# Last groups of a graph layer taken half by half, and products of zeros moved to another bank

## The chip, the cores and the metric

One core of one Trainium2 chip runs the whole kernel. The metric is the device time of one execution in microseconds (us); the median of three runs of the kernel before is 2110.1 us (2109.29 to 2110.33).

The engines, by the short names of the profile: PE multiplies matrices (PEld loads its weights), DVE works on vectors, ACT applies functions, POOL issues the gathers from memory, SP issues the other transfers. Each engine takes its instructions strictly in the order in which they were written for it. Between engines, an instruction waits for semaphores: the end of a write that it needs, or the end of the last use of a buffer that it is to overwrite.

## The reference

Two layers of graph attention with a normalisation ahead and two dense layers behind, added to the input: 6250 nodes with 768 numbers each, 100000 edges sorted by their destination, and one loop edge for each node.

```
h = relu(layernorm(x))
h = relu(gat_conv(h, src, dst, W1, a_src1, a_dst1, b1, heads=4))   # layer 1, 768 -> 256
h = relu(gat_conv(h, src, dst, W2, a_src2, a_dst2, b2, heads=1))   # layer 2, 256 -> 256
h = relu(h @ Wm1 + bm1)
out = x + (h @ Wm2 + bm2)

def gat_conv(x, src, dst, W, a_src, a_dst, bias, heads):
    h = (x @ W).reshape(n, heads, -1)
    alpha_s, alpha_d = (h * a_src).sum(-1), (h * a_dst).sum(-1)
    e = leaky_relu(alpha_s[src] + alpha_d[dst], 0.2)
    e = exp(e - segment_max(e, dst)[dst])
    alpha = e / (segment_sum(e, dst)[dst] + 1e-16)
    return segment_sum(h[src] * alpha[:, :, None], dst) + bias
```

## The kernel before

The 6250 nodes are 49 tiles of 128 (NT = 49). The 100000 edges are 782 tiles of 128, the last with 32 edges. Four edge tiles make a *group* (TPG = 4; NG = 196 groups, numbers 0 to 195, and group 195 has only two tiles), two tiles of a group a *half* or pair, and two groups a *sum* (NU = 98 sums, numbers 0 to 97), which is one accumulation in a bank of PE's result memory, `o_ps`. Such banks rotate: the tag "o" has three of them. Layer 1 is computed first, then layer 2, and nothing of the change touches layer 1.

What layer 2 does with one group, in `group`: POOL has gathered, for each edge, the row of its source node into `G` (256 features, the exponentials of its score, a one for the denominator). DVE has made `hot`, which is 1 where edge and destination match (`make_hot`, L704, for the next group or the next but one). `rho_ps` holds a row per destination, one of four slots for each sum, written by PE (`meet`, L720). In the whole form DVE multiplies `rho_ps` by a column of `G` into `u_ps` (L773), takes the maximum with another column (L775), both for two tiles at a time, and multiplies `hot` by `u_ps` for all four (L778): five instructions. Then PE adds the four products hot x G into the sum (L780). In the other form (`last=True`) it goes tile by tile: one instruction multiplies and takes the maximum (L767), one multiplies `hot` (L769), and that tile's product can follow.

Around it, for each group g, the loop writes `pair(g, 0)`, then one step of the dense layers of earlier nodes, the taking up of a sum, `make_hot` for a later group, other steps, and then `pair(g, 1)`. In layer 2 `pair` runs `group` on the whole group at p == 1 and does nothing at p == 0, but for the last two groups, 194 and 195. `take_sum` (L818, `acc`) reads a finished sum from its bank and adds what it shares with the sum before it; two sums finish a node tile on ACT (L827). Which sum is taken up where stands in UP_AT by hand: sum 95 after the first half of group 192. A node tile then goes through `Node2.steps`: add the loop edge (L1143), divide by the denominator (L1155, L1158), transpose (L1001), ACT (L1007), first dense layer (L1167), ACT (L1172), second dense layer in two parts of 384 columns (L1116 adds the bias, L1177), each part added to x by DVE (L1181), and out. One bank `y_ps` serves both parts in turn, so that PE starts the second when DVE has read the first.

The end is written out in `last_pairs`: sum 96 is taken up, then PE multiplies zeros (`stay_warm`, L902) into the two slots of `rho_ps` that sums 96 and 97 don't use, the halves of groups 194 and 195 follow, and between them the steps of the last two node tiles, 47 (`before`) and 48 (`last`).

Of the kernel before, what the change touches and what calls it, by code (L numbers as in the profile page):

```python
# [10 lines left out]
F32 = mybir.dt.float32  # L11
# [6 lines left out]
P = 128  # L18
# [12 lines left out]
NG = NQ  # L31
# [5 lines left out]
NU = NG // 2  # L37
# [34 lines left out]
def kernel(  # L72
# [21 lines left out]
    nc = tc.nc  # L94
# [9 lines left out]
    ps = edges_stack.enter_context(tc.tile_pool(name="ps", bufs=2, space=bass.MemoryType.PSUM))  # L104
# [28 lines left out]
    idle = const.tile([P, 4 * P], BF16, name="idle")  # L133
# [507 lines left out]
    def layer_edges(layer, H, node, pre, matched, pre_pool):  # L641
# [4 lines left out]
        with tc.tile_pool(name=f"eg{layer}", bufs=6) as eg, \  # L646
# [7 lines left out]
            else:  # L654
                u_ps = ps.tile([P, TPG, P], F32, name="u_ps", tag="factors", bufs=1)
                rho_ps = ps.tile([P, 4, P], F32, name="rho_ps", tag="parts", bufs=1)

            def tiles(g):

                return range(max(TPG * g, FIRST) - TPG * g, min(TPG * g + TPG, LAST) - TPG * g)  # L660
# [89 lines left out]
            def sums_of(u):  # L750

                if u not in o_ps:
                    o_ps[u] = ps.tile([P, RW[layer]], F32, name="o_ps", tag="o", bufs=3)
                return o_ps[u]

            def group(g, of, last=False):

                of = [k for k in of if k in tiles(g)]
                if not of:
                    return  # L760
                u, pairs = g // 2, sorted({k // 2 for k in of})
                row = rho_ps[:, u % 4]
                Gs = {p: G.pop(TPG // 2 * g + p) for p in pairs}
                if last:
                    for k in of:
                        Gk = Gs[k // 2][:, k % 2]
                        nc.vector.tensor_scalar(u_ps[:, k], row, Gk[:, HID + 2:], Gk[:, HID:HID + 1],  # L767
                                                ALU.mult, ALU.max)
                        nc.vector.tensor_mul(hot[g][:, k], hot[g][:, k], u_ps[:, k])  # L769
                else:  # L770
                    for p in pairs:
                        at = slice(2 * p, 2 * p + 2)
                        nc.vector.tensor_mul(u_ps[:, at], row.unsqueeze(1).to_broadcast([P, 2, P]),  # L773
                                             Gs[p][:, :, HID + 2:].to_broadcast([P, 2, P]))
                        nc.vector.tensor_max(u_ps[:, at], u_ps[:, at],  # L775
                                             Gs[p][:, :, HID:HID + 1].to_broadcast([P, 2, P]))
                    at = slice(of[0], of[-1] + 1)
                    nc.vector.tensor_mul(hot[g][:, at], hot[g][:, at], u_ps[:, at])  # L778
                for k in of:
                    nc.tensor.matmul(sums_of(u), hot[g][:, k], Gs[k // 2][:, k % 2, :RW[2]],  # L780
                                     start=(g % 2 == 0 and k == 0),
                                     stop=(g % 2 == 1 and k == tiles(g)[-1]))

            def pair(g, p):

                if layer == 2:
                    if g >= NG - 2:
                        group(g, (2 * p, 2 * p + 1), True)
                    elif p == 1:
                        group(g, range(TPG))  # L790
                    return
                if 2 * p not in tiles(g):
                    return
                Gp = G.pop(TPG // 2 * g + p)
                e1, e2 = Gp[:, :, RW[1]:RW[1] + 4], Gp[:, :, RW[1] + 4:]
                at = TPG * (g % 4) + 2 * p
                rho, v, w = (e_ps[g // 4][:, at:at + 2, k * H:(k + 1) * H] for k in range(3))
                nc.vector.tensor_mul(v, e2, rho)  # L798
                nc.vector.tensor_max(w, v, e1)  # L799
                hw = hwp.tile([P, 2, H, C + 1], F32, name="hw")  # L800
                nc.vector.tensor_mul(  # L801
                    hw, Gp[:, :, :RW[1]].rearrange("p t (h c) -> p t h c", h=H),
                    w.unsqueeze(3).to_broadcast([P, 2, H, C + 1]))
                for t in range(2):
                    k = 2 * p + t
                    nc.tensor.matmul(sums_of(g // 2), hot[g][:, k], hw[:, t].rearrange("p h c -> p (h c)"),  # L806
                                     start=(g % 2 == 0 and k == 0),
                                     stop=(g % 2 == 1 and k == tiles(g)[-1]))
# [3 lines left out]
            def take_sum(u):  # L812

                acc = sums.tile([P, RW[layer]], F32, name="acc")
                if u == 0:
                    nc.vector.tensor_copy(acc, o_ps.pop(u))
                else:
                    nc.vector.scalar_tensor_tensor(acc, run[0], keep[:, u % 2:u % 2 + 1],  # L818
                                                   o_ps.pop(u), ALU.mult, ALU.add)
                for Q in (2 * u - 1, 2 * u):  # L820
                    t, q = divmod(Q, 4)
                    if not 0 <= t < NT - 1:
                        continue
                    if q == 0:
                        done[t] = sums.tile([P, RW[layer]], F32, name="sum", bufs=3)
                    r = slice(32 * q, 32 * q + 32)
                    nc.scalar.activation(done[t][r], acc[r], AF.Copy)  # L827
                    if q == 3:
                        late.append(node.steps(t, done.pop(t)))
                        begun[late[-1]] = t  # L830
                run[0] = acc
                return acc

            def carry_over(acc):

                nc.vector.memset(acc[96:], 0.0)
                run[0] = node.whole(NT - 1, acc)
# [56 lines left out]

            def last_pairs():

                free = 2 * (1 - (NU - 1) % 4 // 2)
                idle_ps = rho_ps[:, free:free + 2].rearrange("p u n -> p (u n)")

                def stay_warm(n):  # L900
                    for _ in range(2 * n):
                        nc.tensor.matmul(idle_ps, idle[:, :P], idle[:, :2 * P], start=True, stop=True)  # L902

                acc = take_sum(NU - 2)
                before, = late
                stay_warm(8)
                pair(NG - 2, 0)
                next(before)
                carry_over(acc)
                next(before)  # L910
                stay_warm(2)
                next(before)
                pair(NG - 2, 1)
                next(before)
                pair(NG - 1, 0)
                pair(NG - 1, 1)
                last = node.steps(NT - 1, None, run[0], o_ps.pop(NU - 1))
                for of in (last, before, last, before, last, before, before, last, last):
                    next(of, 0)
                late.clear()  # L920

            for g in range(NG):
                t, j = divmod(g, 4)
                if layer == 2 and g >= NG - 2:
                    if g == NG - 2:
                        last_pairs()
                    continue
# [594 lines left out]
```

## Time and profile before

| | |
|---|---|
| median of three runs | 2110.1 us (2109.29 to 2110.33) |
| the profiled execution | 2106.61 us, of it 2104.6 us span from the first to the last instruction |
| PE busy | 1649.6 us, 78% of the span |
| DVE busy | 1609.2 us, 76% |
| POOL busy | 1527.1 us, 73% |
| ACT busy | 442.3 us, 21% |
| granted PE clock, mean | 0.917 |

In the rows of the profile a line gives the start in us from the first instruction, the time that the instructions took, the engine, the line of the kernel, the operation, what is written from what, and how many stand together; in square brackets the engine's idle time just before, and what ended it. A matrix product of fp32 numbers appears as two MATMUL records, so that "x8" is four products of a group. Most of the time is spent in the two loops over the groups; the part that this change touches is the last 45 us.

### The profile page before, as it was taken

The page shows a single profiled execution, that of the slowest core. Times are in us where ns is not written, and L with a number is a line of the kernel's source. Part 1 is how long each engine was busy: PE and PEld are TensorE (multiplying, and loading weights), DVE is VectorE, ACT ScalarE, POOL GpSimd, SP SyncE. Part 2 cuts the span into 40 slices and gives each one's busy share as a digit, 9 for nine tenths or more (in the row PEclk, how much of TensorE's full clock was granted, in tenths as well). Part 3 has the DMA queues.
Part 4 walks back from the last instruction along what each step waited for, and adds up shares of the span by engine and source line. Part 5 has one row for each costly group of instructions (what it writes and reads, how often), then busy time and mean ns, then how long its engine had stood idle before and what let it go on. Part 6 is the DMA issues. An engine that isn't in the chain of part 4 may idle for free.

```text
span 2104.6 us, 24738 instructions
## 1 busy us (share of the span) xinstructions
PE 1649.6 (78%) x7217; PEld 1217.7 (58%) x7218; DVE 1609.2 (76%) x3795; ACT 442.3 (21%) x1388; POOL 1527.1 (73%) x1666
## 2 busy tenths in 40 slices
PE   8986879877887887887763787777877777776776
PEld 6875657655665665665542555555555555554554
DVE  7857788887888888888773877777877777776764
ACT  5761111111111111111120111111211111121211
POOL 7067777777777777777777777777777777777773
PEclk9997999998998999999885999998999999999898
DMA  9998455555555556555447355555545555554552
GB/s 349 348 347 286 143 157 155 157 147 155 162 155 149 156 156 161 151 147 161 132 124 215 107 159 159 146 149 159 149 147 159 159 146 149 159 152 137 153 162 77
DMA packets 145655, 354.68 MB, mean 169 GB/s; under 512 B 33943, under 2 KB 57582, under 8 KB 145510
## 3 DMA queue, kind: packets, MB, share of 16 engines
q0 software_dynamic: 75040, 210.90, 37.1%
q1 hardware_dynamic: 69100, 140.62, 19.9%
q10 hardware_dynamic: 1370, 1.48, 0.3%
q8 instruction: 59, 0.97, 0.2%
q14 instruction: 86, 0.70, 0.1%
HBM read 311.29 MB, written 41.59 MB: 168 GB/s over the span
## 4 chain that ended last, share of the span: by engine, by line
DVE 29%; PE 27%; DMA 23%; issue 12%; POOL 7%; ACT 1%; DVEq 0%; SPq 0%; POOLq 0%; ACTq 0%
DMA G<-table,src_i 20%; PE o_ps L780 11%; POOL G L679 7%; DVE u_ps L773 5%; DVE u_ps L775 5%; PE h_ps L471 4%; DVE hw L801 4%; DVE hot L704 4%; DVE hot L778 3%; PE y_ps L1177 2%; PE tp L1167 2%; PE missing L329 2%; DVE soon_hit L318 2%; PE o_ps L806 2%; PE missing L394 2%
## 5 line engine op out<-in xcount | busy, mean ns | idle before, releaser
L679 POOL DMA_INDIRECT G<-table,src_i x1498 | 1426.9, 953 | 456.3 <-issue 266.2
L780 PE MATMUL o_ps<-G,hot 128*128 128x258 f32 x1564 | 445.9, 435 | 245.9 <-DVE hot L778 244.8
L806 PE MATMUL o_ps<-hw,hot 128*128 128x260 f32 x1564 | 457.6, 431 | 170.4 <-DVE hw L801 152.5
L780 PEld LDWEIGHTS o_ps<-G,hot 128*128 128x128 f32 x1564 | 319.5, 213 | 366.1 <-DVE hot L778 313.6
L806 PEld LDWEIGHTS o_ps<-hw,hot 128*128 128x128 f32 x1564 | 302.4, 206 | 284.9 <-DVE hw L801 212.1
L827 ACT ACTIVATE sum<-acc 32x260 f32<-32x260 f32 (+1 forms) x384 | 160.0, 417 | 1345.4 <-DVE acc L818 1286.1
L773 DVE TENSOR_TENSOR u_ps<-rho_ps,G 128x256 f32<-128x256 f32 x388 | 166.5, 429 | 183.8 <-PE rho_ps L720 98.9
L801 DVE TENSOR_TENSOR hw<-G,factors 128x520 f32<-128x520 f32 x391 | 272.1, 696 | 41.3 <-DVE factors L799 2.3
L704 DVE TENSOR_TENSOR hot<-iota_ps,dcol 128x512 f32<-128x512 f32 x392 | 266.0, 679 | 0.0
L329 PE MATMUL missing<-kept,soon_hit 128*128 128x268 f32 x1028 | 246.6, 397 | 0.0
L329 PEld LDWEIGHTS missing<-kept,soon_hit 128*128 128x128 f32 x1028 | 199.8, 196 | 37.5
L775 DVE TENSOR_TENSOR u_ps<-u_ps,G 128x256 f32<-128x256 f32 x388 | 167.7, 432 | 13.4
L1177 PE MATMUL y_ps<-wm,mT 128*128 128x384 f32 x392 | 153.1, 514 | 0.3 <-ACT mT L1172 0.3
L798 DVE TENSOR_TENSOR factors<-G,factors 128x8 f32<-128x8 f32 x391 | 65.0, 166 | 102.8 <-DMA G<-table,src_i 98.5
L471 PE MATMUL h_ps<-w,r 128*128 128x264 f32 (+1 forms) x588 | 137.4, 387 | 7.2 <-ACT r L461 7.0
L778 DVE TENSOR_TENSOR hot<-hot,u_ps 128x512 f32<-128x512 f32 x194 | 133.1, 686 | 6.7
L471 PEld LDWEIGHTS h_ps<-w,r 128*128 128x128 f32 x588 | 107.8, 190 | 29.4 <-ACT r L461 10.6
L292 POOL DMA_INDIRECT G<-table,soon_i x46 | 44.0, 957 | 74.5 <-DMA xt<-in_x 53.0
L818 DVE SCALAR_TENSOR_TENSOR acc<-acc,keep,o_ps 128x260 f32<-128x260 f32 (+1 forms) x192 | 91.5, 477 | 7.8 <-PE o_ps L780 7.8
L1177 PEld LDWEIGHTS y_ps<-wm,mT 128*128 128x128 f32 x392 | 67.0, 191 | 44.3 <-issue 17.4
L799 DVE TENSOR_TENSOR factors<-factors,G 128x8 f32<-128x8 f32 x391 | 68.0, 174 | 13.6 <-DVE factors L798 0.2
L1181 DVE TENSOR_TENSOR y<-y_ps,xt 128x384 f32<-128x384 f32 (+1 forms) x98 | 54.0, 551 | 29.1 <-PE y_ps L1177 28.9
(426 smaller groups left out, 1367.9 us busy)
## 6 DMA issues: line engine op xcount, KB each, us to landing
xt<-in_x SPq DMA_DIRECT2D x96, 384.0 KB, 5.3
drow<-dmod_d SPq DMA_DIRECT2D x49, 512.0 KB, 5.2
G<-table,src_i POOLq DMA_INDIRECT x1498
xTt<-in_xT SPq DMA_DIRECT2D x49, 384.0 KB, 7.5
out<-y SPq DMA_DIRECT2D x48, 384.0 KB, 3.1
table<-kept SPq DMA_DIRECT2D x49, 134.0 KB, 5.3
table<-kept SPq DMA_DIRECT2D x49, 129.5 KB, 2.7
soon_d<-G SPq DMA_DIRECT2D x23, 268.0 KB, 7.9
```

Source lines behind the costliest of these rows:

```text
L329: nc.tensor.matmul(soon_p[k], hit[:, T - there], kept[T], start=(T == there), stop=(T == NT - 1))
L471: nc.tensor.matmul(h_ps[:, :n], r[:, k], w1[:, k, :n], start=(k == 0), stop=(k == KI - 1))
L679: nc.gpsimd.indirect_dma_start(out=G[k // 2][:n, k % 2], out_offset=None, in_=table[layer], in_offset=bass.IndirectOffsetOnAxis(ap=src_i[: ...
L704: nc.vector.tensor_tensor(hot[g][:, T[0]:T[0] + n], iota_ps.unsqueeze(1).to_broadcast([P, n, P]), dcol[:, k:k + n].unsqueeze(2).to_broadca ...
L773: nc.vector.tensor_mul(u_ps[:, at], row.unsqueeze(1).to_broadcast([P, 2, P]), Gs[p][:, :, HID + 2:].to_broadcast([P, 2, P]))
L775: nc.vector.tensor_max(u_ps[:, at], u_ps[:, at], Gs[p][:, :, HID:HID + 1].to_broadcast([P, 2, P]))
L778: nc.vector.tensor_mul(hot[g][:, at], hot[g][:, at], u_ps[:, at])
L780: nc.tensor.matmul(sums_of(u), hot[g][:, k], Gs[k // 2][:, k % 2, :RW[2]], start=(g % 2 == 0 and k == 0), stop=(g % 2 == 1 and k == tiles( ...
L801: nc.vector.tensor_mul(hw, Gp[:, :, :RW[1]].rearrange("p t (h c) -> p t h c", h=H), w.unsqueeze(3).to_broadcast([P, 2, H, C + 1]))
L806: nc.tensor.matmul(sums_of(g // 2), hot[g][:, k], hw[:, t].rearrange("p h c -> p (h c)"), start=(g % 2 == 0 and k == 0), stop=(g % 2 == 1 ...
L827: nc.scalar.activation(done[t][r], acc[r], AF.Copy)
L1177: nc.tensor.matmul(y_ps, mT[:, j], wm2[:, j, s * half:(s + 1) * half], start=False, stop=(j == KH - 1))
```

## The change

The whole diff:

```
-                    if g >= NG - 2:
+                    if g >= NG - 4:
                         group(g, (2 * p, 2 * p + 1), True)
                     elif p == 1:
                         group(g, range(TPG))
...
             def last_pairs():
 
-                free = 2 * (1 - (NU - 1) % 4 // 2)
-                idle_ps = rho_ps[:, free:free + 2].rearrange("p u n -> p (u n)")
+                idle_ps = ps.tile([P, 4 * P], F32, name="idle_ps", tag="o", bufs=3)
 
                 def stay_warm(n):
-                    for _ in range(2 * n):
-                        nc.tensor.matmul(idle_ps, idle[:, :P], idle[:, :2 * P], start=True, stop=True)
+                    for _ in range(n):
+                        nc.tensor.matmul(idle_ps, idle[:, :P], idle, start=True, stop=True)
```

Groups 192 and 193 are now also done in halves, tile by tile. The first half of group 192 comes ahead of the taking up of sum 95 and of two `make_hot`, and its products come ahead of the second dense layer of node tile 46 on PE. The products of zeros write to a bank of the tag "o", which is no longer a part of `rho_ps`; each is 512 columns wide in place of 256, and there are half as many. Because two lines are gone, the lines behind them have numbers that are lower by one.

Three places of the order of instructions follow. The names: `hot_15632` and `G_15581`, `G_15586` belong to group 192, `hot_15676` before and `hot_15683` now with `G_15654`, `G_15659` to group 194; `o_ps_15604` is sum 95; L1181 (now L1180) is the addition of x for node tiles 45 and 46. What a row waits for stands in brackets: DMASW is the gathers, DMAHW other transfers.

DVE around group 192, before:

```order
L1181 TENSOR_TENSOR y_15574<-y_ps_15575,xt_15404 128x384 [waits PE_49]
L818 SCALAR_TENSOR_TENSOR acc_15670<-acc_15589,keep_86,o_ps_15604 128x258 [waits PE_49]
L704 TENSOR_TENSOR hot_15674<-iota_ps_77,dcol_94 128x512
L704 TENSOR_TENSOR hot_15676<-iota_ps_77,dcol_94 128x512
L773 TENSOR_TENSOR u_ps_9898<-rho_ps_9899,G_15581 128x256 [waits DMASW7_49,DMASW6_49,DVE_49]
L775 TENSOR_TENSOR u_ps_9898<-u_ps_9898,G_15581 128x256 [waits DVE_49]
L773 TENSOR_TENSOR u_ps_9898<-rho_ps_9899,G_15586 128x256 [waits DMASW1_49,DMASW0_49,DVE_49]
L775 TENSOR_TENSOR u_ps_9898<-u_ps_9898,G_15586 128x256 [waits DVE_49]
L778 TENSOR_TENSOR hot_15632<-hot_15632,u_ps_9898 128x512 [waits DVE_49]
L1181 TENSOR_TENSOR y_15665<-y_ps_15666,xt_15521 128x384 [waits DMAHW6_49,DMAHW4_49,PE_49]
L678 MEMSET G_15694 128x259
L1181 TENSOR_TENSOR y_15665<-y_ps_15666,xt_15521 128x384 [waits PE_49]
```

The same twelve places of DVE now:

```order
L1180 TENSOR_TENSOR y_15574<-y_ps_15575,xt_15404 128x384 [waits PE_49]
L767 TENSOR_SCALAR u_ps_9898<-rho_ps_9899,G_15581 128x128 [waits DMASW6_49,DVE_49]
L769 TENSOR_TENSOR hot_15632<-hot_15632,u_ps_9898 128x128 [waits DVE_49]
L767 TENSOR_SCALAR u_ps_9898<-rho_ps_9899,G_15581 128x128 [waits DMASW7_49,DVE_49]
L769 TENSOR_TENSOR hot_15632<-hot_15632,u_ps_9898 128x128 [waits DVE_49]
L818 SCALAR_TENSOR_TENSOR acc_15677<-acc_15589,keep_86,o_ps_15604 128x258 [waits PE_49]
L704 TENSOR_TENSOR hot_15681<-iota_ps_77,dcol_94 128x512
L704 TENSOR_TENSOR hot_15683<-iota_ps_77,dcol_94 128x512
L767 TENSOR_SCALAR u_ps_9898<-rho_ps_9899,G_15586 128x128 [waits DMASW0_49,DVE_49]
L769 TENSOR_TENSOR hot_15632<-hot_15632,u_ps_9898 128x128 [waits DVE_49]
L767 TENSOR_SCALAR u_ps_9898<-rho_ps_9899,G_15586 128x128 [waits DMASW1_49,DVE_49]
L769 TENSOR_TENSOR hot_15632<-hot_15632,u_ps_9898 128x128 [waits DVE_49]
```

Five instructions on a whole group have become twice four on single tiles; the first four stand ahead of the taking up of sum 95 (L818), the others behind both `make_hot` (L704) and ahead of the addition of x.

PE around group 192, before (`o_ps_15683` before and `o_ps_15666` now are sum 96, `y_ps_15666` and `y_ps_15673` the second dense layer of node tile 46):

```order
L1167 MATMUL tp_15629<-rT_15645,wm1_9850 128x128 [waits Activation_49]
L1167 MATMUL tp_15629<-rT_15645,wm1_9850 128x128 x3
L1116 LDWEIGHTS ones_r_9854
L1116 MATMUL y_ps_15666<-bm2r_9853,ones_r_9854 128x384 [waits DVE_49]
L1177 MATMUL y_ps_15666<-wm2_9851,mT_15662 128x384 [waits Activation_49] x2
L780 MATMUL o_ps_15683<-G_15581,hot_15632 128x258 [waits DMASW6_49,DVE_49]
L780 MATMUL o_ps_15683<-G_15581,hot_15632 128x258 [waits DMASW7_49]
L780 MATMUL o_ps_15683<-G_15586,hot_15632 128x258 [waits DMASW0_49]
L780 MATMUL o_ps_15683<-G_15586,hot_15632 128x258 [waits DMASW1_49]
L1116 LDWEIGHTS ones_r_9854
L1116 MATMUL y_ps_15666<-bm2r_9853,ones_r_9854 128x384 [waits DVE_49]
L1177 MATMUL y_ps_15666<-wm2_9851,mT_15662 128x384 x2
```

PE there now:

```order
L1166 MATMUL tp_15629<-rT_15645,wm1_9850 128x128 [waits Activation_49]
L1166 MATMUL tp_15629<-rT_15645,wm1_9850 128x128 x3
L780 MATMUL o_ps_15666<-G_15581,hot_15632 128x258 [waits DMASW6_49,DVE_49]
L780 MATMUL o_ps_15666<-G_15581,hot_15632 128x258 [waits DMASW7_49,DVE_49]
L1115 LDWEIGHTS ones_r_9854
L1115 MATMUL y_ps_15673<-bm2r_9853,ones_r_9854 128x384
L1176 MATMUL y_ps_15673<-wm2_9851,mT_15669 128x384 [waits Activation_49] x2
L780 MATMUL o_ps_15666<-G_15586,hot_15632 128x258 [waits DMASW0_49,DVE_49]
L780 MATMUL o_ps_15666<-G_15586,hot_15632 128x258 [waits DMASW1_49,DVE_49]
L1115 LDWEIGHTS ones_r_9854
L1115 MATMUL y_ps_15673<-bm2r_9853,ones_r_9854 128x384 [waits DVE_49]
L1176 MATMUL y_ps_15673<-wm2_9851,mT_15669 128x384 x2
```

The group's four products, which stood in one row between the two parts of the second dense layer and waited for the group's one `hot`, are now two ahead of the first part and two between the parts, each waiting for its own tile's `hot`.

DVE from the taking up of sum 96 to the second half of group 194, before:

```order
L818 SCALAR_TENSOR_TENSOR acc_15711<-acc_15670,keep_86,o_ps_15683 128x258 [waits PE_49]
L767 TENSOR_SCALAR u_ps_9898<-rho_ps_9899,G_15654 128x128 [waits DMASW6_49,DVE_49,PE_49]
L769 TENSOR_TENSOR hot_15676<-hot_15676,u_ps_9898 128x128 [waits DVE_49]
L767 TENSOR_SCALAR u_ps_9898<-rho_ps_9899,G_15654 128x128 [waits DMASW7_49,DVE_49]
L769 TENSOR_TENSOR hot_15676<-hot_15676,u_ps_9898 128x128 [waits DVE_49]
L1143 SCALAR_TENSOR_TENSOR all__15737<-kept47_162,own_9961,sum_15592 128x258 [waits Activation_49]
L1155 RECIPROCAL rden_15739<-all__15737 128x1 [waits DVE_49]
L836 MEMSET acc_15711 32x258
L1143 SCALAR_TENSOR_TENSOR all__15742<-kept48_163,own_9961,acc_15711 128x258 [waits DVE_49]
L767 TENSOR_SCALAR u_ps_9898<-rho_ps_9899,G_15659 128x128 [waits DMASW0_49,PE_49]
```

The same ten places now:

```order
L818 SCALAR_TENSOR_TENSOR acc_15718<-acc_15677,keep_86,o_ps_15666 128x258 [waits PE_49]
L767 TENSOR_SCALAR u_ps_9898<-rho_ps_9899,G_15654 128x128 [waits DMASW6_49,DVE_49]
L769 TENSOR_TENSOR hot_15683<-hot_15683,u_ps_9898 128x128 [waits DVE_49]
L767 TENSOR_SCALAR u_ps_9898<-rho_ps_9899,G_15654 128x128 [waits DMASW7_49,DVE_49]
L769 TENSOR_TENSOR hot_15683<-hot_15683,u_ps_9898 128x128 [waits DVE_49]
L1142 SCALAR_TENSOR_TENSOR all__15736<-kept47_162,own_9961,sum_15592 128x258 [waits Activation_49]
L1154 RECIPROCAL rden_15738<-all__15736 128x1 [waits DVE_49]
L836 MEMSET acc_15718 32x258
L1142 SCALAR_TENSOR_TENSOR all__15741<-kept48_163,own_9961,acc_15718 128x258 [waits DVE_49]
L767 TENSOR_SCALAR u_ps_9898<-rho_ps_9899,G_15659 128x128 [waits DMASW0_49]
```

The order is the same; the two reads of `rho_ps` by L767 that waited for PE as well now wait only for their gathers and for DVE's own work.

## The prediction

> **What bounds the kernel now.** The change touches only the end, so I read the timeline of the last 45 us first, then what DVE and PE waited for there, then the granted clock by windows, last the gathers. The first fence is the page's span, the second the timeline from group 192 to the products of group 193.
>
> ```profile
> span 2104.6 us, 24738 instructions
> ```
>
> ```profile
> 2062.26 0.56 DVE L1181 TENSOR_TENSOR y<-y_ps,xt 128x384 f32<-128x384 f32 x1 [1.36 <-PE y_ps L1177]
> 2062.28 1.91 PE L780 MATMUL o_ps<-G,hot 128*128 128x258 f32 x8
> ...
> 2064.02 1.05 PE L1167 MATMUL tp<-rT,wm 128*128 128x128 f32 x8
> 2064.22 0.48 DVE L818 SCALAR_TENSOR_TENSOR acc<-acc,keep,o_ps 128x258 f32<-128x258 f32 x1 [1.40 <-PE o_ps L780]
> 2064.62 1.28 DVE L704 TENSOR_TENSOR hot<-iota_ps,dcol 128x512 f32<-128x512 f32 x2
> ...
> 2065.00 0.33 PE L1116 MATMUL y_ps<-bm2r,ones_r 3*128 3x384 bf16 x1
> ...
> 2065.59 1.56 PE L1177 MATMUL y_ps<-wm,mT 128*128 128x384 f32 x4 [0.25 <-ACT mT L1172]
> 2065.82 0.42 DVE L773 TENSOR_TENSOR u_ps<-rho_ps,G 128x256 f32<-128x256 f32 x1
> ...
> 2068.42 2.01 PE L780 MATMUL o_ps<-G,hot 128*128 128x258 f32 x8 [1.27 <-DVE hot L778]
> ...
> 2068.83 0.27 DVE L678 MEMSET G<- 128x259 f32 x1
> ...
> 2070.62 1.56 PE L1177 MATMUL y_ps<-wm,mT 128*128 128x384 f32 x4
> ...
> 2072.21 0.56 DVE L1181 TENSOR_TENSOR y<-y_ps,xt 128x384 f32<-128x384 f32 x1 [3.11 <-PE y_ps L1177]
> 2072.69 0.41 DVE L704 TENSOR_TENSOR hot<-iota_ps,dcol 128x256 f32<-128x256 f32 x1
> ...
> 2075.62 3.81 PE L780 MATMUL o_ps<-G,hot 128*128 128x258 f32 x8 [3.44 <-DVE hot L778]
> ```
>
> DVE and PE work here in turn, not side by side. PE waits 1.27 us for the whole of group 192, multiplies for 2.01 us and goes on with node tile 46; DVE meanwhile has an addition of x in front (L1181) that waits 3.11 us for that, and only behind it group 193; PE waits 3.44 us for this. The four products of group 193 then take 3.81 us where group 192's took 2.01.
>
> The next fence is the timeline from there to the last sum.
>
> ```profile
> 2079.22 2.85 PE L902 MATMUL rho_ps<-idle 128*128 128x256 bf16 x16
> ...
> 2079.46 0.48 DVE L818 SCALAR_TENSOR_TENSOR acc<-acc,keep,o_ps 128x258 f32<-128x258 f32 x1 [3.90 <-PE o_ps L780]
> ...
> 2082.11 0.42 DVE L767 TENSOR_SCALAR u_ps<-rho_ps,G 128x128 f32<-128x128 f32 x1 [2.16 <-PE rho_ps L902]
> ...
> 2083.54 0.48 DVE L1143 SCALAR_TENSOR_TENSOR all__15737<-kept,own,sum 128x258 f32<-128x258 f32 x1
> ...
> 2084.64 0.49 DVE L1143 SCALAR_TENSOR_TENSOR all__15742<-kept,own,acc 128x258 f32<-128x258 f32 x1
> 2084.87 0.20 PEld L1001 LDWEIGHTS tp<-ident,o 128*128 128x128 f32 x2 [0.90 <-ACT o L1158]
> ...
> 2085.79 0.42 DVE L767 TENSOR_SCALAR u_ps<-rho_ps,G 128x128 f32<-128x128 f32 x1 [0.66 <-PE rho_ps L902]
> ...
> 2086.09 1.16 PE L1167 MATMUL tp<-rT,wm 128*128 128x128 f32 x8 [0.34 <-ACT rT L1007]
> ...
> 2086.56 0.42 DVE L767 TENSOR_SCALAR u_ps<-rho_ps,G 128x128 f32<-128x128 f32 x1
> ...
> 2087.01 0.29 DVE L769 TENSOR_TENSOR hot<-hot,u_ps 128x128 f32<-128x128 f32 x1
> ...
> 2087.34 0.42 DVE L767 TENSOR_SCALAR u_ps<-rho_ps,G 128x128 f32<-128x128 f32 x1
> ...
> 2088.56 0.29 DVE L769 TENSOR_TENSOR hot<-hot,u_ps 128x128 f32<-128x128 f32 x1
> ...
> 2089.71 0.42 DVE L1153 TENSOR_TENSOR all__15778<-all__15742,o_ps 128x258 f32<-128x258 f32 x1 [0.86 <-PE o_ps L780]
> ```
>
> Sum 96 is taken up at 2079.46. DVE could go on at once, but reads `rho_ps`, into which PE multiplies zeros: it waits 2.16 us, and 0.66 us more behind the second stretch of zeros. From 2082.11 to 2089.71 DVE sets the pace, with 0.86 us for the last products; the last 14.9 us (2089.71 to 2104.6) are one chain of node tile 48 and its way out.
>
> The granted clock, in windows of 3.41 us. Columns: window, its length, busy time of PE, PEld, DVE, ACT, POOL, then PEclk.
>
> ```profile
> 2036.76:2040.17 3.41, 1.63 (x6) 0.75 (x6) 2.60 (x6) 0.00 (x0) 2.50 (x4) 1.00 0.40 120
> 2053.83:2057.24 3.41, 1.52 (x6) 0.75 (x5) 3.27 (x8) 0.76 (x2) 2.50 (x4) 1.00 0.41 116
> 2057.24:2060.65 3.41, 3.41 (x9) 1.97 (x7) 3.24 (x9) 0.51 (x1) 2.79 (x3) 0.50 0.44 115
> 2070.89:2074.30 3.41, 1.29 (x4) 0.40 (x3) 2.02 (x5) 0.00 (x0) 1.81 (x2) 1.00 0.45 134
> 2074.30:2077.71 3.41, 2.09 (x5) 1.72 (x6) 1.19 (x3) 0.00 (x0) 0.00 (x0) 0.50 0.18 74
> 2077.71:2081.13 3.42, 3.42 (x13) 2.31 (x13) 0.48 (x1) 0.41 (x1) 0.00 (x0) 0.50 0.00 0
> ```
>
> A window with 1.29 or 1.52 us of PE work is followed by one at half clock; one with 1.63 us wasn't. So group 193's products and the zeros ran at 0.50 because PE had stood idle from 2072.18 to 2075.62.
>
> **The change, part by part.** I walk DVE and PE through the new order with these rows' distances. A tile in the new form takes 0.78 us of DVE (2086.56, 2087.01, 2087.34), a half 1.56, a group 3.12. The old form needs 2.60 (2065.82 to PE's start at 2068.42). So each of two groups costs DVE 0.52 us more, in all 1.04; the gain must come from overlap. Two products take PE about 0.95 (half of 1.91 to 2.01).
>
> *Group 192.* DVE's first half follows the addition at 2062.26 (0.5 later): 2062.75 to 2064.3. Sum 95 can't be taken up before 2064.22 anyway, so 0.1 is lost; with 0.4 and 1.2 for L818 and L704 x2, the second half runs from 2065.9 to 2067.5. PE's two products go in at 2065.0 in front of L1116, so the first part of the dense layer ends near 2067.7 (0.95 + 0.26 + 1.5), the next products at 2068.6, the second part (L1116 from there, 1.76) at 2070.4. Queued behind DVE's addition, which now waits 0.3 us (2067.75), is group 193.
>
> *Group 193.* Memset and first half: 2068.25 to 2070.05. The addition waits for PE until 2070.4, then the short `make_hot` (0.33): second half 2071.3 to 2072.85. PE does the first two products at 2070.4 to 2071.3, the third at 2072.1, the last from 2072.9. Sum 96 is taken up at 2073.45 in place of 2079.46: **6.0 us**.
>
> *The zeros.* Their bank is the one from which sum 94 was taken long before, so nothing waits for it; the bias products that later reuse it (second L1116 of node tile 48) come behind them on PE itself. DVE's two waits go: **2.16 and 0.66 us**. Late next on DVE is nothing until 195's products. For 512 columns the end of the trace has no row; the nearest is from the kernel's start, at clock 1.00:
>
> ```profile
> 7.71 1.89 PE L508 MATMUL warm_ps<-idle 128*128 128x512 bf16 x8
> ```
>
> So `stay_warm(8)` takes 1.89 us there; the other end is 2.85 us, the same columns at 2079.22 mostly at 0.50. I take 1.89: PE is free at 2075.2, and DVE has group 194's first half ready at 2075.4 (2073.85 + 1.56), so it is hidden. With 2.85 it would show for 0.8 us.
>
> *The end.* L1143 comes at 2075.4 (was 2083.54), the second L1143 is done 1.59 later at 2077.0 (2084.64 + 0.49 before), the last `hot` 3.06 later at 2080.05 (was 2088.85). PE: transposes 1.33 behind L1143 (2084.87 before) at 2076.7, L1167 1.22 later at 2077.9 and done at 2079.1, group 194's last products until 2080.0, L1116, then 195's until 2081.1. L1153 starts at 2081.1, which is 8.6 before 2089.71: 6.0 + 2.16 + 0.66 = 8.8, less 0.2 because PE, not DVE, is now last by a little. The rest of the chain is untouched.
>
> POOL gets no other instruction, SP and ACT none either. The gathers must be there: issue times of group 192's second tile and of the last tile, and the longest way to landing that I found in the chain.
>
> ```profile
> 2057.20 0.95 POOL L679 DMA_INDIRECT G<-table,src_i  x1 [0.30 <-issue]
> ...
> 2072.18 0.87 POOL L679 DMA_INDIRECT G<-table,src_i  x1 [0.30 <-issue]
> ```
>
> ```profile
> 1849.59 5.35 DMA G<-table,src_i
> ```
>
> Even with 5.35 us they are there at 2062.55 and 2077.5; DVE asks for them at 2063.5 and 2079.3.
>
> Clock: in the windows 2070.89 to 2074.30 and on to 2077.71 my walk gives PE 2.3 and 2.8 us of work, far over the 1.52 that made it fall; so the sum is made at 1.00. The Trainium skill ("TensorE: Matmul & The Clock Gate", section "What's actually happening") lets the clock fall only after a whole idle window of about 3.4 us. The rows disagree, 1.52 us of work in the window didn't save it, and they decide; the sum is 8.6 by either, but by the page the first rival below would have no chance.
>
> So 2104.6 - 8.6 = 2096.0 of span; with the 2.0 us around it (2106.61 - 2104.6) 2098.0 for the profiled execution. That execution was 3.5 us below the median 2110.1; I take the gain from the median: 2101.5.
>
> **Rivals.**
> *The clock falls all the same* at 2074.30, since PE is now fed in twos with gaps. For it: it fell at 2057.24 too, with PE 45% busy. Against it: the gaps are 0.8 us at most. Price: half the zeros at half clock (PE free at 2075.9), 194's products 1.9 (half of 3.81) to 2077.8, transposes to 2078.6, L1167 from 2080.1 to 2081.9, and 2.2 for the rest: L1153 at 2084.1, gain 5.6, 2104.5. The Trainium skill (same page, section "A second HAM failure mode: psum-queue depth-cycling") tells of a kernel whose PE idles shortly between groups of products and whose clock goes to and fro; that speaks against the twos, but no window here with so much work shows it. Lasting to the end, it would also double the PE work behind:
>
> ```profile
> 2092.70 1.05 PE L1167 MATMUL tp<-rT,wm 128*128 128x128 f32 x8
> ...
> 2093.59 3.53 PE L1177 MATMUL y_ps<-wm,mT 128*128 128x384 f32 x10
> ```
>
> With the transposes and bias that is some 5.5 us, and 2.4 more ahead of L1153: 2112.5, within the band of no change.
> *Slower: half clock from group 192 on.* The PE work on the path of groups 192 and 193 (6 us) doubles as well: 2118. It decides only where more than 8.6 us of path work run at half clock. Against it: PE works nearly without pause from 2062 to 2071.
> *Gathers late*: if landings took 2 us more than the longest row, the first half of group 192 would hold DVE's queue for 1.8 us: gain 6.8, 2103.3.
> *The zeros still hold DVE back*: then 1.89 and 0.5 us of waits remain and 6.6 are gained, 2103.5; the order shows no such wait.
>
> **How the numbers follow.** Forecast 0.82, its own range 2099.8 to 2103.0 (products and zeros between the bounds above); clock falling once 0.07; to the end 0.05; from group 192 on 0.03; late gathers 0.02; waits that stay 0.01. A measurement of this kernel can tell about 0.2%, 4.2 us, from no change. Faster: 0.82 + 0.07 + 0.03 = 0.92, same 0.05, slower 0.03. The range of 8 in 10 takes in the forecast's own and the clock falling once: 2099.8 to 2105.0.
>
> **What would show it.** L818 of sum 96 near 2073.4; no wait of L767 for PE; PEclk at 1.00 to the end; L780 of group 193 in pieces, none over 1.1 us a pair; L1152 (L1153 before) near 2081, with 15 us from there to the end as before. Wrong: half clock behind 2074, DVE waiting for gathers in group 192, or an addition of x (L1180) that waits over 1 us.

## The result, and the profile after

| | before | changed |
|---|---|---|
| median of the first runs (7 and 7) | 2109.71 us | 2103.55 us (2100.08 to 2105.72) |
| ratio, 95% interval | | 0.997 (0.996 to 0.9979) |
| median of a second set (24 and 5) | 2106.65 us | 2097.28 us (2096.35 to 2102.43) |
| ratio, 95% interval | | 0.9958 (0.9944 to 0.9971) |
| profiled execution | 2106.61 us | 2104.75 us |
| *the end*, in the profiles | 42.3 us | 33.9 and 33.8 us |

The changed kernel is faster, by 6.2 us in the first runs (2101.5 was forecast, and 2103.55 lies in the range of 2099.8 to 2105.0) and by 9.4 us in the second set. The ratios, here and below, are taken over those executions that are at most 1.5% above the fastest of their kernel in the set. *The end* is my measure for the rest of the text: from the start of the addition of x that stands ahead of group 192 on DVE (2062.26 before) to the last instruction. The order ahead of it is the same in the two kernels.

The page's first line after the change, and the timeline of DVE and PE through the same places as before:

```profile
span 2102.7 us, 24732 instructions
```

```profile
2068.77 0.55 DVE L1180 TENSOR_TENSOR y<-y_ps,xt 128x384 f32<-128x384 f32 x1
...
2069.24 0.41 DVE L767 TENSOR_SCALAR u_ps<-rho_ps,G 128x128 f32<-128x128 f32 x1
...
2070.95 0.48 DVE L818 SCALAR_TENSOR_TENSOR acc<-acc,keep,o_ps 128x258 f32<-128x258 f32 x1 [0.21 <-PE o_ps L780]
...
2071.64 1.04 PE L780 MATMUL o_ps<-G,hot 128*128 128x258 f32 x4
...
2074.27 1.03 PE L780 MATMUL o_ps<-G,hot 128*128 128x258 f32 x4
...
2074.47 0.56 DVE L1180 TENSOR_TENSOR y<-y_ps,xt 128x384 f32<-128x384 f32 x1 [0.41 <-PE y_ps L1176]
...
2076.89 1.03 PE L780 MATMUL o_ps<-G,hot 128*128 128x258 f32 x4
...
2077.09 0.56 DVE L1180 TENSOR_TENSOR y<-y_ps,xt 128x384 f32<-128x384 f32 x1 [0.50 <-PE y_ps L1176]
...
2078.68 1.48 PE L780 MATMUL o_ps<-G,hot 128*128 128x258 f32 x4 [0.76 <-DVE hot L769]
...
2080.20 0.48 DVE L818 SCALAR_TENSOR_TENSOR acc<-acc,keep,o_ps 128x258 f32<-128x258 f32 x1 [0.80 <-PE o_ps L780]
2080.21 1.67 PE L901 MATMUL idle_ps<-idle 128*128 128x512 bf16 x7
2080.60 0.41 DVE L767 TENSOR_SCALAR u_ps<-rho_ps,G 128x128 f32<-128x128 f32 x1
...
2083.52 0.41 DVE L767 TENSOR_SCALAR u_ps<-rho_ps,G 128x128 f32<-128x128 f32 x1
...
2088.04 0.42 DVE L1152 TENSOR_TENSOR all__15775<-all__15741,o_ps 128x258 f32<-128x258 f32 x1 [1.45 <-PE o_ps L780]
```

The four products of a group, two L780 records each, now come in twos of 1.03 us that lie beside DVE's halves; only the last two of group 193 take 1.48 us together, because the second waits for its tile (the prediction had said that no pair would take over 1.1). The additions of x wait 0.41 and 0.50 us for PE, where one waited 3.11. Sum 96 is taken up 11.4 us behind the first row (17.2 before), the first L767 of group 194 follows 0.40 later with no wait for PE (2.65 later before), and so does the one at 2083.52. L1152 comes 19.3 us behind the first row, L1153 came 27.45 behind.

The granted clock in stretches of 3.40 us of the changed kernel's end, laid without regard to the clock's own windows, columns as before:

```profile
2071.00:2074.40 3.40, 3.40 (x18) 2.31 (x17) 2.95 (x7) 1.46 (x4) 2.52 (x3) 1.00 0.55 160
2074.40:2077.80 3.40, 3.40 (x14) 1.97 (x12) 2.73 (x8) 0.00 (x0) 2.76 (x3) 1.00 0.42 112
2077.80:2081.20 3.40, 2.51 (x10) 1.28 (x11) 2.46 (x8) 0.41 (x1) 0.00 (x1) 1.00 0.39 140
2081.20:2084.60 3.40, 2.56 (x13) 1.18 (x10) 3.08 (x10) 1.13 (x3) 0.00 (x0) 1.00 0.00 0
```

PE is busy for at least 2.51 us of each, and the clock stays at 1.00. The two later profiles of this kernel show the same in the clock's own windows: at least 2.53 and 2.57 us of work in each from group 192 to the last sum, and 1.00 until PE's last product.

The end is 8.4 us shorter in this profile, but the execution is only 1.9 us shorter, because the first row comes at 2068.77 instead of 2062.26. The last gather, from the timeline of POOL:

```profile
2076.94 0.87 POOL L679 DMA_INDIRECT G<-table,src_i  x1 [0.30 <-DVE hot L769]
```

It was issued at 2072.18 before. So POOL was already 4.8 of these 6.5 us later in this execution, in instructions that both kernels share; in the second profile of the changed kernel it came at 2074.56. The other 1.7 us lie between POOL and DVE: the start of the end comes 9.9 us ahead of the last gather's issue before, and 8.2 here. In the six profiles of the first two sets of runs that distance is anything from 8.0 to 10.8 us.

### The profile page after: what moved, and what is told of

Its sections match the earlier page's. It is cut to its first block, busy times and chain, and to the rows that moved or that the text cites. A ratio compares the mean times of both kernels' runs of the same rounds, so it can differ in the third digit from the quotient of the medians.

```text
span 2102.7 us, 24732 instructions
## 1 busy us (share of the span) xinstructions
PE 1670.2 (79%) x7206; PEld 1233.1 (59%) x7208; DVE 1608.9 (77%) x3801; ACT 442.7 (21%) x1388; POOL 1531.1 (73%) x1666
## 3 DMA queue, kind: packets, MB, share of 16 engines
q10 hardware_dynamic: 1370, 1.48, 0.3%
## 4 chain that ended last, share of the span: by engine, by line
DVE 28%; DMA 26%; PE 25%; issue 12%; POOL 8%; ACT 1%; DVEq 0%; SPq 0%; POOLq 0%; ACTq 0%
DMA G<-table,src_i 23%; PE o_ps L780 11%; POOL G L679 7%; DVE u_ps L773 4%; PE h_ps L471 4%; DVE u_ps L775 4%; DVE hw L801 4%; DVE hot L704 3%; DVE hot L778 3%; PE y_ps L1176 3%; PE tp L1166 2%; DVE soon_hit L318 2%; PE missing L394 2%; DVE factors L799 1%; DVE factors L798 1%
## 5 line engine op out<-in xcount | busy, mean ns | idle before, releaser
L780 PE MATMUL o_ps<-G,hot 128*128 128x258 f32 x1564 | 458.5, 445 | 230.1 <-DVE hot L778 228.9
L806 PE MATMUL o_ps<-hw,hot 128*128 128x260 f32 x1564 | 462.5, 435 | 165.9 <-DVE hw L801 148.5
L780 PEld LDWEIGHTS o_ps<-G,hot 128*128 128x128 f32 x1564 | 329.5, 219 | 350.9 <-DVE hot L778 294.1
L773 DVE TENSOR_TENSOR u_ps<-rho_ps,G 128x256 f32<-128x256 f32 x384 | 164.7, 429 | 184.8 <-PE rho_ps L720 98.9
L801 DVE TENSOR_TENSOR hw<-G,factors 128x520 f32<-128x520 f32 x391 | 272.1, 696 | 41.3 <-DVE factors L799 2.3
L704 DVE TENSOR_TENSOR hot<-iota_ps,dcol 128x512 f32<-128x512 f32 x392 | 266.0, 679 | 0.0
L818 DVE SCALAR_TENSOR_TENSOR acc<-acc,keep,o_ps 128x260 f32<-128x260 f32 (+1 forms) x192 | 91.5, 477 | 4.8 <-PE o_ps L780 4.8
L1180 DVE TENSOR_TENSOR y<-y_ps,xt 128x384 f32<-128x384 f32 (+1 forms) x98 | 54.1, 552 | 28.0 <-PE y_ps L1176 27.9
```

Source lines behind the costliest of these rows:

```text
L704: nc.vector.tensor_tensor(hot[g][:, T[0]:T[0] + n], iota_ps.unsqueeze(1).to_broadcast([P, n, P]), dcol[:, k:k + n].unsqueeze(2).to_broadca ...
L801: nc.vector.tensor_mul(hw, Gp[:, :, :RW[1]].rearrange("p t (h c) -> p t h c", h=H), w.unsqueeze(3).to_broadcast([P, 2, H, C + 1]))
```

## The experiments

All ends in one table. The start is that of the addition of x ahead of group 192 (L1181, or its line in that kernel), the end is the span.

| kernel | start | span | the end | sum 96 taken up, behind the start |
|---|---|---|---|---|
| before, first profile | 2062.26 | 2104.6 | 42.3 | 17.2 |
| before, second and third profile | 2511.66, 2536.88 | 2553.0, 2579.2 | 41.3, 42.3 | 17.0, 17.4 |
| changed, three profiles | 2068.77, 2066.58, 2513.83 | 2102.7, 2100.4, 2547.5 | 33.9, 33.8, 33.7 | 11.4, 11.2, 11.4 |
| halves alone | 2062.59 | 2098.2 | 35.6 | 11.4 |
| bank alone | 2063.43 | 2103.2 | 39.8 | 17.0 |
| changed, no zeros | 2064.39 | 2100.2 | 35.8 | 11.4 |
| changed, sixteen zeros | 2504.80 | 2539.9 | 35.1 | 11.4 |
| changed, 8 groups in halves | 2521.09, 2519.38 | 2554.2, 2552.6 | 33.1, 33.2 | 10.6 |
| 24 groups, all groups | 2528.85, 2506.06 | 2562.1, 2539.5 | 33.2, 33.4 | 10.6 |

The runs came in four sets: the first runs, a second set (before 2106.65 us), a third and a fourth. In the third (the kernel before again, sixteen zeros, 8 groups) and the fourth (changed once more, 8, 24 and all groups) the kernel before took 2569 us instead of 2107. In its profile there L773, which can wait only for gathers, PE and DVE, waited 217 us for something that the profile can't name; gathers that landed late are the likely cause, but this is not shown. From these two sets I use ends and ratios, and no difference from the first two.

Inside the end DVE waited for no gather in any of these profiles, so an end holds the work of DVE, PE and ACT alone. Counted from the last gather's issue instead, it is 32.4 us before, 25.8 in both profiles of the changed kernel of the first two sets, 24.8 with the halves alone, 30.6 with the bank alone and 25.8 without zeros. By that mark the halves alone are no worse than the full change; but it holds as well the 8.0 to 10.8 us by which DVE's start lay ahead of the last gather, which differed from execution to execution.

**The halves alone.** The zeros go to `rho_ps` as before.

```
-                    if g >= NG - 2:
+                    if g >= NG - 4:
```

> The end is counted from the start of the addition of x ahead of group 192 on DVE to the last instruction: 42.3 us before, 33.9 us after. Theory of waits (DVE and PE side by side in groups 192 and 193, and DVE's two waits for the zeros in rho_ps, each worth its own time): the halves alone keep the waits, 16 products of zeros at full clock are about 2.3 us and the second wait 0.66 us, so the end is about 36.4 us, and the median about 2.5 us above that of the full change. Theory of the clock (the end before was long because PE fell to half clock at 2074.30, and the halves keep it awake): the halves alone give all of it, end about 34.5 us, and the median within 1 us of the full change.

Median 2100.8 us (11 runs), ratio to the kernel before 0.9973 (0.9964 to 0.9982). The timeline from the taking up of sum 96:

```profile
2073.81 1.91 PE L902 MATMUL rho_ps<-idle 128*128 128x256 bf16 x16
2074.01 0.48 DVE L818 SCALAR_TENSOR_TENSOR acc<-acc,keep,o_ps 128x258 f32<-128x258 f32 x1 [0.80 <-PE o_ps L780]
...
2075.76 0.42 DVE L767 TENSOR_SCALAR u_ps<-rho_ps,G 128x128 f32<-128x128 f32 x1 [1.27 <-PE rho_ps L902]
...
2079.44 0.42 DVE L767 TENSOR_SCALAR u_ps<-rho_ps,G 128x128 f32<-128x128 f32 x1 [0.66 <-PE rho_ps L902]
```

The waits are still there, 1.27 + 0.66 = 1.9 us, and the end is 1.7 to 1.8 us longer than with the full change (35.6 against 33.8 to 33.9). The waits are as the theory of waits said, but 35.6 lies between its 36.4 and the 34.5 of the theory of the clock, because the first wait is 0.9 shorter than it was (2.16): the sixteen products ran at full clock in 1.91 us, not in 2.85. So 0.9 us of the wait that the bank was credited with was half clock. The median is 3.5 us above that of the full change in the same set (2097.28), which points the same way, though the two intervals overlap.

**The bank alone.** Groups 192 and 193 whole.

```
-                    if g >= NG - 4:
+                    if g >= NG - 2:
```

> The zeros in a bank of their own, groups 192 and 193 whole as before. Theory of waits: DVE's 2.16 and 0.66 us of waiting go, but PE is busy with zeros until about the same time and comes 0.5 us later than DVE would, so the end is about 40 us in place of 42.3, and the median 2 to 2.5 us below the kernel before. Theory of the clock: the products of group 193 and the zeros are still at half clock in some executions, PE is last, and the end gains under 1 us.

Median 2105.93 us (11 runs), ratio 1.0 (0.9991 to 1.0009). From the timeline:

```profile
2077.01 3.42 PE L780 MATMUL o_ps<-G,hot 128*128 128x258 f32 x8 [3.44 <-DVE hot L778]
...
2080.47 0.48 DVE L818 SCALAR_TENSOR_TENSOR acc<-acc,keep,o_ps 128x258 f32<-128x258 f32 x1 [3.51 <-PE o_ps L780]
2080.48 1.67 PE L901 MATMUL idle_ps<-idle 128*128 128x512 bf16 x7
2080.86 0.41 DVE L767 TENSOR_SCALAR u_ps<-rho_ps,G 128x128 f32<-128x128 f32 x1
...
2088.31 0.42 DVE L1152 TENSOR_TENSOR all__15769<-all__15735,o_ps 128x258 f32<-128x258 f32 x1 [1.46 <-PE o_ps L780]
```

DVE goes on 0.39 us behind L818, the waits are gone, the 3.44 us of PE's waiting and the slow products of group 193 are left (3.42 us, 3.81 before). The end is 39.8, as the theory of waits said, 2.5 below the first profile of before. The times don't show it: the interval allows 1.9 us either way. Against the other end seen before (41.3, below) the gain is 1.5, which the interval allows; how much the bank alone is worth over many executions stays open between 0 and 1.9 us.

**No zeros at all.** Both calls of `stay_warm` are left out; their products are used nowhere.

```
-                stay_warm(8)
...
-                stay_warm(2)
```

> The full change with all products of zeros left out (they compute nothing that is used). Theory of waits: they are hidden beside DVE's first half of group 194, the end stays within 0.5 us of 33.9 and the median within 1 us of the full change. Theory of the clock: without them PE works under 1.6 us in one window of 3.41 us, the granted clock falls to 0.50 behind it, and the end grows by 3 us or more.

Median 2101.14 us (8 runs), ratio 0.9977 (0.9967 to 0.9988). Two rows of the timeline and the windows:

```profile
2077.00 2.09 PE L780 MATMUL o_ps<-G,hot 128*128 128x258 f32 x4 [1.22 <-DVE hot L769]
...
2080.44 2.07 PE L1164 MATMUL tp<-rT,wm 128*128 128x128 f32 x8 [0.77 <-ACT rT L1004]
```

```profile
2073.04:2076.45 3.41, 1.90 (x7) 0.69 (x5) 2.51 (x8) 0.12 (x1) 1.81 (x2) 1.00 0.64 205
2076.45:2079.87 3.42, 2.66 (x6) 1.38 (x6) 3.10 (x10) 0.91 (x3) 0.00 (x0) 0.50 0.01 2
2079.87:2083.28 3.41, 2.84 (x11) 2.66 (x12) 2.12 (x7) 1.19 (x4) 0.00 (x0) 0.50 0.00 0
2083.28:2086.69 3.41, 3.32 (x13) 1.82 (x12) 0.80 (x3) 0.51 (x2) 0.00 (x0) 1.00 0.01 2
```

The clock falls for two windows, L1164 takes 2.07 us in place of 1.16, and the end is 1.9 to 2.1 us longer than the change's. So the theory of waits missed here: the zeros, hidden though they are, keep the clock up. The rival's 3 us was too much. One profile shows it; other executions, with other windows, may lose less. The times point the same way: the median is 3.9 us above that of the full change in the same set (8 and 5 runs), and the two intervals overlap a little.

**The changed kernel again.**

> The changed kernel unaltered, for a second profile and more times beside these. If the code ahead of group 192, which is the same, costs the same, the median is 8 us below the kernel before, as the end is (42.3 against 33.9). If the end before is on average shorter than in its one profile, because the windows of the clock fall otherwise in other executions, the median stays 5 to 7 us below, and the profile shows an end near 33.9 again at another position of the windows.

Ratio 0.9958 (0.9944 to 0.9971), 9.4 us between the medians; the end is 33.8. Both sets' intervals hold the 8.4 us by which the end is shorter (4.4 to 8.4 at 2107 us, and 6.1 to 11.8), the first at its upper edge. So the times need no loss ahead of group 192. They don't decide between the two explanations of the expectation either: 9.4 is nearer to the first, 6.2 to the second, and the next two runs show that the end before is indeed shorter in some executions.

**The kernel before again**, twice.

> The kernel before, unaltered, for a second profile. Its one profile had an end of 42.3 us with 6.83 us at half clock (2074.30 to 2081.13). Theory of waits: the end is the same within 0.5 us wherever the windows of the clock fall. Theory of the clock: the windows fall otherwise in each execution, PE is at half clock for 3.4 us or not at all in the end, and the end lies anywhere from 40 to 42.5 us.

> The kernel before once more, a third profile, with the same expectations as the second: an end of 42.3 us within 0.5 us by the theory of waits, anywhere from 40 to 42.5 us by the theory of the clock.

The second profile, first rows of the timeline and then windows:

```profile
2525.24 3.39 PE L780 MATMUL o_ps<-G,hot 128*128 128x258 f32 x8 [3.44 <-DVE hot L778]
...
2528.47 1.91 PE L902 MATMUL rho_ps<-idle 128*128 128x256 bf16 x16
...
2530.42 0.42 DVE L767 TENSOR_SCALAR u_ps<-rho_ps,G 128x128 f32<-128x128 f32 x1 [1.26 <-PE rho_ps L902]
```

```profile
2521.26:2524.67 3.41, 0.54 (x2) 0.00 (x0) 2.69 (x7) 0.00 (x0) 0.00 (x0) 1.00 0.31 118
2524.67:2528.08 3.41, 2.84 (x7) 2.28 (x8) 0.52 (x1) 0.00 (x0) 0.00 (x0) 0.50 0.00 0
2528.08:2531.50 3.42, 2.59 (x20) 2.00 (x19) 1.49 (x4) 0.41 (x1) 0.00 (x0) 1.00 0.00 0
```

Here the windows fell so that PE was at half clock for one of them only, the zeros ran at full clock, and the end is 41.3. The third profile is like the first: 2.94 us of zeros, a wait of 2.25, an end of 42.3. So the end before depends on where the windows lie, by 1.0 us in three profiles; the theory of the clock is right to that extent, and the change's gain is 7.4 to 8.6 us (41.3 or 42.3 less 33.7 to 33.9).

This also settles why the halves' 6.7 us and the bank's 2.5 don't add up to the 8.4 of both. The bank alone had one window at half clock, like the second profile of before, and its zeros ran at full clock. Against that profile's 41.3 the halves alone gain 5.7, the bank alone 1.5 and both together 7.4 to 7.6: there they nearly add up. The overlap is 0.9 us of zeros at half clock in the first profile of before, which neither run of one part alone had, so that both are credited with it.

**Sixteen products of zeros** in place of eight.

```
-                stay_warm(8)
+                stay_warm(16)
```

> The full change with sixteen products of zeros in place of eight at the taking up of sum 96. Theory of waits: eight are hidden beside DVE's first half of group 194 with little to spare, the other eight are 1.9 us of PE at full clock, of which PE's own later waits take up some: the end is 1.3 to 1.7 us longer (35.1 to 35.6). Theory of the clock: more zeros keep PE awake and cost nothing, end 33.9.

The end is 35.1, at the lower edge of the theory of waits. The rows of the first and the last piece:

```profile
2516.25 3.40 PE L901 MATMUL idle_ps<-idle 128*128 128x512 bf16 x15
...
2524.98 0.42 DVE L1152 TENSOR_TENSOR all__15783<-all__15749,o_ps 128x258 f32<-128x258 f32 x1 [2.35 <-PE o_ps L780]
```

1.73 us more of zeros (3.40 against 1.67) make DVE's last wait 0.9 us longer (2.35 against 1.45) and the end 1.2 to 1.4 longer. So of the added 1.73 us only 0.3 to 0.5 were hidden: eight is near the number that fits beside DVE's two tiles, though no other number was tried.

**More groups in halves**: 8, 24, all 196.

```
-                    if g >= NG - 4:
+                    if g >= NG - 8:
```

> The full change with the last eight groups in halves in place of the last four. If DVE and PE side by side is what pays, groups 188 to 191 pay too, as long as DVE comes later than the gathers: the time from the last gather's issue to the end (25.8 us in both profiles of the change, 32.4 before) falls by up to 3 us, and the median by 1 to 3 us below the changed kernel. If DVE's 0.52 us more for each group is what counts ahead of the end, where POOL issues a group every 5.0 us and DVE is 70 to 80% busy, it is the same or slower by up to 2 us.

> The changed kernel unaltered once more, as the comparison for the kernels with more groups in halves, on the same chip: 6 to 9 us below the kernel before, time from the last gather's issue to the end 25 to 26 us if the gathers keep their 1.25 us pace.

> The last eight groups in halves (four in the change). If DVE and PE side by side pays in groups 188 to 191 too, because DVE comes later than the gathers there, the time from the last gather's issue to the end falls by up to 3 us from the 25.8 of the change, and the median is 1 to 3 us below the changed kernel beside it. If the gathers set when these groups can start, both are within 1 us of the change.

> The last 24 groups in halves. If what halves win is the delay of DVE and PE behind the gathers, it can be won once only, near the end: the same as with eight, within 1 us. If DVE's 0.52 us more for each group counts, 16 more groups cost up to 8 us, less what POOL's pace (a group every 5.0 us against some 4.2 of DVE) hides: 0 to 3 us slower than with eight.

> All groups of layer 2 in halves. DVE is 75% busy in layer 2 before (149 to 154 us in 200), and 0.52 us more for each group of 5.0 us makes it 85 to 87%. If POOL's pace still sets the loop, the time is within 3 us of the kernel with 24 groups in halves. If DVE's waits for PE leave it too little, the loop falls behind POOL: up to 100 us slower (196 groups of 0.52 us).

| kernel | median (12 runs) | ratio to before | 95% interval |
|---|---|---|---|
| 8 groups, third set | 2556.48 us | 0.9886 | 0.9837 to 0.9934 |
| changed, fourth set | 2559.0 us | 0.9973 | 0.9938 to 1.0008 |
| 8 groups, fourth set | 2552.88 us | 0.9957 | 0.9925 to 0.9988 |
| 24 groups, fourth set | 2562.96 us | 0.997 | 0.993 to 1.001 |
| all groups, fourth set | 2544.45 us | 0.9935 | 0.9896 to 0.9973 |

The 2556.48 in the third set is the median of executions from 2518.54 to 2571.46, of which six enter the ratio; hence a ratio so much lower than that of the same kernel in the fourth set. The end shrinks by 0.3 to 0.6 us (33.7 to between 33.1 and 33.4), and no further with more groups; but with these kernels the groups just ahead of it differ too. By the expectations' own measure, the time from the last gather's issue, nothing is won: 27.1 and 27.2 us with 8 groups, 27.3 with 24 and 27.4 with all, against 26.9 of the changed kernel in the fourth set, where up to 3 less were possible. That measure is a poor one here, because the last issue waited some 30 us for DVE in each of these profiles. The times can't decide between differences of 1 to 3 us: the changed kernel itself isn't clear of the kernel before in the fourth set (0.9938 to 1.0008). The 102 us that 196 groups at 0.52 would cost DVE don't show in the time: all groups in halves is no slower than the change, although DVE's busy time in the whole kernel is 1661.1 us instead of 1600.8. The windows of that kernel:

```profile
1900.00:2100.00 200.00, 147.70 (x518) 92.17 (x517) 140.39 (x378) 31.41 (x84) 127.78 (x136) 0.86 0.46 129
2100.00:2300.00 200.00, 142.12 (x484) 88.08 (x483) 133.06 (x359) 30.03 (x80) 125.43 (x133) 0.83 0.43 123
```

DVE is busy for 133 to 140 us in 200, so it has room, in executions this long. Whether all groups in halves also beats the change stays open: the fourth set's intervals overlap, the same kernel with 8 groups gave 0.9886 and 0.9957, and the first two sets don't have it.

## Why the prediction was right

- *Halves side by side with PE*: sum 96 was forecast 11.2 us behind the start (2073.45 - 2062.26); it came at 11.4 and 11.2. The term of 6.0 us measured 5.8 and 6.0. The halves alone shorten the end by 6.7 us. The name says too little, though: the prediction walked PE at full clock, and group 193's four products, 2.0 us at full clock, took 3.81 us in the first profile of before and 3.39 in the second. By these rows 1.4 to 1.8 us of the term are clock and about 4 are overlap; no run has the one without the other.
- *DVE's waits for the zeros*: both are gone, as the order of instructions said. The term of 2.16 + 0.66 less 0.2 was 2.6; from the taking up of sum 96 to L1153 the change saves 2.4 (10.25 to 7.84). The price of the waits was read from one execution: 0.9 us of the first was half clock, which went with the halves alone (1.27 us left) and also in the second profile of before, without any change (1.26). For the rival in which the waits stay, the prediction's 6.6 us doesn't follow from its own terms (8.8 less 2.4 is 6.4); the halves alone, which are that case, gained 6.7 with waits of 1.27 and 0.66.
- *Eight zeros hidden*: right, 1.67 us for the seven records that the profile has of the eight, and the sixteen show that more are not.
- *The clock*: 1.00 until PE's last product in the three profiles of the change. The first rival did not happen there; it happened without the zeros, at 1.9 to 2.1 us in place of the 3.0 priced. Behind that stood the rule that PE work of over 1.52 us in a window keeps the clock up, and this failed: 1.90 us in 2073.04 to 2076.45 did not (above). It did no harm, because the change has at least 2.5 us in each window. The Trainium skill ("TensorE: Matmul & The Clock Gate", section "What's actually happening") gives one idle window or more as what brings the slow clock back; the trace disagrees, as PE worked 1.90 of 3.41 us there. The Trainium skill (same page, section "A second HAM failure mode: psum-queue depth-cycling") tells of short idle times between groups of products at which the clock goes to and fro. The change, with its twos of products, shows none of that (1.00 in all three ends); the kernel without zeros comes nearer to it, with one fall of two windows.
- *Gathers*: no wait of DVE for them at group 192 or behind in the change, as worked out.
- *What sets the pace behind the zeros*: the prediction said DVE, from 2082.11 to 2089.71. The chain that ended last runs through DVE only until 2084.31 and then through ACT and PE, the transposes and L1167 of node tile 47 (2084.87 to 2087.24) and the last products. It cost the sum little: 2.4 of the 2.6 us came.
- *The sum*: 8.6 forecast, 8.4 in the profile's end and 7.4 to 8.6 over the profiles. That the first median showed 6.2 is partly luck of the range: 2103.55 lies above the forecast's own range (2099.8 to 2103.0), in the part that had been added for a fall of the clock, which no profile of the change shows. The 8.4 is at the upper edge of that set's interval (4.4 to 8.4). Two things can make the median differ from the sum: the end before was priced from one profile and is 1.0 shorter in another, and the last gather alone moved by 4.8 us between two executions. Which of them did is not shown.

## What to carry to other kernels

Where two engines work in turn at a kernel's end, cut the work into halves that hand over early; it pays even if the halves cost more in sum, and it shows as long as nothing else (here the gathers) decides when they start. Give filler work a buffer that no one else reads (1.5 to 1.8 us of the end here, though the times of the bank alone show nothing), and count it as clock, not as waste: it was free beside DVE, and leaving it out cost 2 us in the one profile without it. Measure such a change on a stretch between two marks in the profile when executions differ by more than it is worth, make sure that nothing outside is waited for between the marks, and take more than one profile: the end before was 42.3, 41.3 and 42.3 us.

## What the runs showed of the hardware

The clock's windows of 3.41 us lie otherwise from the first instruction in each execution (boundaries at 2074.30 in one profile of before, 2076.45 and 2083.28 in one without zeros, 2524.67 in another of before), and the same idle time costs one window at half clock or two. How much work in a window keeps the clock up is not settled by PE's busy time: 1.63 us did once and 1.90 didn't. To bring it back took more: windows at half clock with 2.09 and 2.66 us of PE work were followed by another at half clock, those with 2.84 us (two profiles) by one at full clock.
